# Three queues for the transfers of the last convolution: stores on SyncE and GpSimd, image loads on ScalarE

## The chip, the cores and the metric

The kernel runs on one core of one Trainium2 chip. The metric is the device time of one execution in microseconds (us), the median of several runs; smaller is better. A profiled execution gives the trace from which everything else is read.

## What is computed

The input x has 8 images of 16 channels of 256 x 256 float32. Four layers follow one another, each of the form x = x + f(gn(x)), where gn normalizes pairs of channels (8 groups of 2): a convolution with capsule routing, a convolution of splines, an attention over 16 x 16 patches, and last a 3 x 3 convolution with circular padding that the reference writes as a product of Fourier transforms. Only the last layer is touched here:

```
# --- layer 3 (conv_preact) ---
x = x + _L3_conv_ref(_gn(x), L3_conv_weight)
```

Because the padding is circular and the normalization is one factor and one offset for each image and channel, the layer is one convolution for each image: the factor goes into the weights, with 1 added at the centre for the residual, and the offset goes into a bias.

## The kernel before

The program is written instruction by instruction for each engine: TensorE (PE), VectorE (DVE), ScalarE (ACT), GpSimd (POOL) and SyncE (SP). A scheduler adds semaphores where one instruction needs another's result. In the last layer the order on each engine is the order of the program text (a manual schedule).

**Data.** The layer before writes its result to a scratch tensor in DRAM, `self.x3[b]`, one for each image `b`. `fetch3` (L1466) loads one image into an SBUF tile `xs` of 128 partitions x 33 x 258 floats with three DMAs: two of 2064 KB (L1471) and one of 32 KB (L1472). Three tiles take turns: `x30` (the profile calls it `pt`, since it is shared with the layer before) and two tiles `x3s`. Image 0 is loaded by SyncE during the layer before. Images 1 and 2 are loaded when the last layer begins, and image n + 2 into the tile of image n - 1, by an instruction that stands between the two halves of image n.

**Work.** For each image `n` there are two steps, s = 0 and s = 2; each step makes half of the image's rows and fills one tile `y` (`y3`, four buffers). In a step `products` (L1512) runs four times: q = 0 for k = 0 and 1, then q = 1 for k = 0 and 1. One such call is 48 products of 32 x 32 weights with 512 columns in float32, which the trace shows as 96 instructions MATMUL and 96 weight loads; a step is 384 of each. Two copies `seen` (L1583), one by ScalarE and one by VectorE, read the result of q = 0. `evict` (L1528) adds the bias and moves the result from PSUM to `y`: ScalarE takes k = 0 (L1537), VectorE takes k = 1 (L1535). The eight banks of PSUM are all in use in a step, so the products of the next step for k = 0 need ScalarE's eviction of this one.

**Stores.** `store` (L1539) writes the tile to the output. Partition 32c + 2o + r of `y` holds channel o of strip c (four strips of 64 rows), row parity r. For each c there are a DMA of 16 channels x 8 pieces of 2 KB (256 KB), one of 16 x 7 pieces of 2 KB (224 KB), and one of 16 x 2 rows of 1 KB (32 KB); in the step s = 2 the last of these for c = 3 is split in two of 16 KB because the image wraps around. So a step has 12 stores (s = 0) or 13 (s = 2), all issued by SyncE at one line, L1545.

**Waits.** A DMA signals its end on a semaphore. The DMAs of SyncE and ScalarE together use eight semaphores in rotation, those of GpSimd eight others; a DMA waits until the earlier one with its semaphore has landed.

The main loop, which sets the order:

```
for n, b in enumerate(images):
    for s in (0, 2):
        y = io.tile([P, 2, 2, 4, W], F32, name="y3", bufs=4)
        if s and n and n + 2 < len(images):
            xs.append(fetch(images[n + 2], xs[n - 1]))
...
        store(b, s, y)
```

Of the kernel before, what the change touches and what calls it, by code (L numbers as in the profile page):

```python
# [17 lines left out]
B, C, H, W = 8, 16, 256, 256  # L18
# [265 lines left out]
class _Net:  # L284
# [1189 lines left out]
    def layer3(self, images=range(B)):  # L1474
# [5 lines left out]
        nc, tc = self.nc, self.tc  # L1480
        with ExitStack() as st:
# [12 lines left out]
                return get  # L1494

            def fetch(b, xs):
                self.fetch3(nc.gpsimd, b, xs)
                return xs

            def weights(b):  # L1500
# [38 lines left out]
            def store(b, s, y):  # L1539

                y = y.rearrange("(c o r) s g j w -> r o c (s g j) w", c=4, r=2)

                def put(row, ap, src):
                    to = self.out[b, 0, row]
                    nc.sync.dma_start(out=bass.AP(tensor=to.tensor, offset=to.offset, ap=[[H * W, C], *ap]), in_=src)  # L1545

                row = 16 * s + 1
                for c in range(4):
                    for r, n in ((1, 8), (0, 7)):
                        put(  # L1550
                            row + 64 * c + 3 - 2 * r,
                            [[4 * W, n], [1, 2 * W]],
                            y[r, :, c, 1 - r : 1 - r + 2 * n].rearrange("o (m t) w -> o m (t w)", t=2),
                        )
                    if row + 64 * c + 31 < H:
                        put(row + 64 * c, [[31 * W, 2], [1, W]], y[0, :, c, 0:16:15])
                    else:
                        put(row + 64 * c, [[W, 1], [1, W]], y[0, :, c, 0:1])
                        put(0, [[W, 1], [1, W]], y[0, :, c, 15:16])
# [3 lines left out]
            xs = [self.x30.rearrange("p (g w) -> p g w", w=WP)]  # L1563
# [3 lines left out]
            with tc.manual_schedule():  # L1567
                for b in images[1:3]:
                    xs.append(fetch(b, io.tile([P, 33, WP], F32, name="x3s")))
# [5 lines that stand above are left out]
                        ps = [[psum.tile([P, 2, 512], F32, name="p3") for _ in range(2)] for _ in range(2)]  # L1575
                        for q in range(2):
                            for k in range(2):
                                products(s + k, q, ws, xs[n], ps[k])
                                if q:
                                    evict(b, s + k, ps[k], y)  # L1580
                                else:
                                    for h in range(2):
                                        (nc.vector.tensor_copy if k else nc.scalar.copy)(  # L1583
                                            seen[k][:, h], ps[k][h][:, :, 0]
                                        )
                        store(b, s, y)
                        if todo:
                            todo.pop(0)[2]()
                        while todo and todo[0][0] != "PE":
                            todo.pop(0)[2]()  # L1590
                        if s == 0 and n + 1 < len(images):
                            ws_after = weights(images[n + 1])
                    if n + 1 < len(images):
                        ws = ws_after
# [69 lines left out]
```

## Time and profile before

| what | value |
|---|---|
| median of 3 runs | 6713.02 us (6710.88 to 6718.76) |
| the profiled execution's own time | 6716.81 us |
| its span, first to last instruction | 6714.9 us |
| the last convolution in it, from the first product to the end | 6450.6 to 6714.9 us |
| TensorE busy over the span | 91% |
| mean granted TensorE clock | 0.985 |
| moved by DMA over the span | 800.86 MB |

The profiled execution lies 3.8 us over the median. Times inside it are counted from the start of the span. "PE" is TensorE's products, "PEld" its weight loads. "SPq" is the queue of SyncE's DMA instructions. The trace names DMA queues by number: q1 is SyncE's, q10 ScalarE's, q0 GpSimd's, and q8 brings the instructions of TensorE from DRAM. A row of the table by stretch of time has, in this order, the stretch and its length, the busy time and number of instructions of PE, PEld, DVE, ACT and POOL, the granted clock, the busy share of the 16 DMA engines and the GB/s moved.

### The profile page before, as it was taken

The page shows a single profiled execution, that of the slowest core. Times are in us where ns is not written, and L with a number is a line of the kernel's source. Part 1 is how long each engine was busy: PE and PEld are TensorE (multiplying, and loading weights), DVE is VectorE, ACT ScalarE, POOL GpSimd, SP SyncE. Part 2 cuts the span into 40 slices and gives each one's busy share as a digit, 9 for nine tenths or more (in the row PEclk, how much of TensorE's full clock was granted, in tenths as well). Part 3 has the DMA queues.
Part 4 walks back from the last instruction along what each step waited for, and adds up shares of the span by engine and source line. Part 5 has one row for each costly group of instructions (what it writes and reads, how often), then busy time and mean ns, then how long its engine had stood idle before and what let it go on. Part 6 is the DMA issues. An engine that isn't in the chain of part 4 may idle for free. (4 is left out here: it accounts for less than half of the span.)

```text
span 6714.9 us, 111421 instructions
## 1 busy us (share of the span) xinstructions
PE 6114.2 (91%) x46024; PEld 2770.4 (41%) x46024; DVE 5401.2 (80%) x6374; ACT 2737.7 (41%) x3898; POOL 3231.7 (48%) x2098
## 2 busy tenths in 40 slices
PE   3899899899988999899887799999999999999988
PEld 1333333333333333333333344444444466666655
DVE  5799999999999999999998899999999633333321
ACT  1333333333333333333332688888888421221211
POOL 0566666666666666666666444334344211111100
PEclk9999999999999999999998899999999999999999
DMA  6233333333333333333332555555556634344358
GB/s 260 61 87 90 92 90 93 90 88 91 91 90 91 89 88 88 88 88 88 88 88 61 171 177 176 175 176 178 175 174 175 177 87 94 81 93 95 91 173 222
DMA packets 375967, 800.86 MB, mean 119 GB/s; under 512 B 56210, under 2 KB 190386, under 8 KB 338210
## 3 DMA queue, kind: packets, MB, share of 16 engines
q1 hardware_dynamic: 339426, 730.09, 38.3%
q10 hardware_dynamic: 33792, 33.82, 1.5%
q0 software_dynamic: 2240, 29.82, 1.2%
q8 instruction: 361, 5.91, 0.4%
q14 instruction: 148, 1.21, 0.1%
HBM read 582.87 MB, written 210.77 MB: 118 GB/s over the span
## 5 line engine op out<-in xcount | busy, mean ns | idle before, releaser
L750 POOL TENSOR_TENSOR dd<-dd 128x1024 f32<-128x1024 f32 x512 | 1214.5, 2372 | 615.9 <-DVE dd L741 595.8
L1006 PE MATMUL ps<-bases,tw 128*32 128x512 f32 (+1 forms) x13824 | 1361.5, 545 | 18.2 <-POOL bases L975 7.9
L741 DVE SCALAR_TENSOR_TENSOR dd<-rb,v 128x1024 f32<-128x1024 f32 (+1 forms) x1024 | 1066.5, 1082 | 97.5 <-PE rb L730 91.0
L975 POOL TENSOR_TENSOR bases<-e,a 128x1024 f32<-128x1024 f32 (+1 forms) x264 | 621.8, 2378 | 930.9 <-DVE e L973 930.6
L629 DVE TENSOR_TENSOR pr<-v,fb 128x2048 f32<-128x2048 f32 (+1 forms) x512 | 1011.5, 2016 | 24.1 <-PE pl L639 12.8
L523 PE MATMUL cv<-kt,w 128*128 128x512 f32 x2048 | 1000.1, 610 | 28.2 <-DVE dd L741 21.4
L532 ACT COPY v<-cv 128x1024 f32<-128x1024 f32 x512 | 517.3, 1010 | 1151.7 <-PE cv L527 1151.7
L1006 PEld LDWEIGHTS ps<-bases,tw 128*32 128x32 f32 x13824 | 596.2, 109 | 804.9 <-issue 484.7
L750 POOL TENSOR_TENSOR s<-s,dd 128x512 f32<-128x512 f32 x512 | 671.4, 1311 | 35.0
L730 PE MATMUL rb<-rs,ct_fold 32*128 32x512 f32 x3584 | 608.9, 649 | 71.4 <-ACT rs L712 68.0
L750 POOL TENSOR_TENSOR s<-v,dd 128x512 f32<-128x512 f32 x256 | 330.3, 1290 | 659.8 <-DVE dd L741 659.8
L639 PE MATMUL pl<-pr,ct_fold 128*32 128x512 f32 x3584 | 534.2, 608 | 120.6 <-DVE pr L629 120.6
L527 PE MATMUL cv<-kt,w 64*128 64x512 f32 x2048 | 578.7, 641 | 0.0
L523 PEld LDWEIGHTS cv<-kt,w 128*128 128x128 f32 x2048 | 354.2, 190 | 524.9 <-issue 300.0
L1430 ACT ACTIVATE vt<-pv,w_b2v 128x128 f32<-128x128 f32 x512 | 146.5, 368 | 842.6 <-PE pv L1426 842.6
L1419 PE MATMUL pqk<-w_qk,t 128*128 128x512 f32 x1024 | 483.0, 594 | 4.6 <-POOL t L1413 4.6
L1451 DVE TENSOR_TENSOR y<-po,res 128x512 f32<-128x512 f32 x128 | 88.5, 692 | 490.8 <-PE po L1446 472.0
L983 DVE SCALAR_TENSOR_TENSOR bases<-xr,xm,bases 128x1024 f32<-128x1024 f32 (+1 forms) x264 | 447.8, 1734 | 0.3 <-POOL bases L975 0.3
L1413 POOL TENSOR_TENSOR t<-t,emb 128x512 f32<-128x512 f32 x128 | 162.3, 1268 | 507.2 <-DVE t L1409 496.5
L960 ACT ACTIVATE sq<-a 128x1024 f32<-128x1024 f32 (+1 forms) x264 | 263.7, 999 | 228.1 <-DVE a L952 227.3
L730 PEld LDWEIGHTS rb<-rs,ct_fold 32*128 32x128 f32 x3584 | 172.9, 185 | 415.6 <-issue 219.9
L942 ACT ACTIVATE d<-xr,bd,sd 128x1024 f32<-128x1024 f32 (+1 forms) x264 | 319.0, 1208 | 20.0 <-DMA xr<-x1p 20.0
(261 smaller groups left out, 8377.6 us busy)
## 6 DMA issues: line engine op xcount, KB each, us to landing
kt<-d SPq DMA_DIRECT2D x256, 516.0 KB
xr<-x1p SPq DMA_DIRECT2D x120, 1024.0 KB
d<-dn ACTq DMA_DIRECT2D x64, 516.0 KB
x<-y SPq DMA_DIRECT2D x128, 258.0 KB
xs<-in_x_dram SPq DMA_DIRECT2D x16, 2048.0 KB
xs<-in_x_dram SPq DMA_DIRECT2D x64, 512.0 KB
res<-in_x_dram SPq DMA_DIRECT2D x64, 512.0 KB
x<-s SPq DMA_DIRECT2D x128, 256.0 KB
```

The costliest lines, as they stand in the source:

```text
L523: nc.tensor.matmul(ps()[:, n], w[:, 0, j, :], t[:, a : a + 2, 0:W], start=True, stop=False)
L527: nc.tensor.matmul(ps()[:, n], w[at, 1, j, :], t[at, a : a + 2, 2 - n : 2 - n + W], start=False, stop=True)
L532: nc.scalar.copy(v[h]()[:, 4 * g : 4 * g + 4, j * W : j * W + W], ps().rearrange("p n (a w) -> p (n a) w", w=W),)
L629: nc.vector.tensor_tensor(pr()[:, :n].rearrange("p n (r w) -> p n r w", w=W), v[h]()[:, 4 * g : 4 * g + n].rearrange("p n (r w) -> p n r w ...
L639: nc.tensor.matmul(pl()[at : at + 32], sel[:, g, h, :], pr()[:, t, :], start=h == 0 and g == 0, stop=h == 1 and (g == 1 or t == 3),)
L730: nc.tensor.matmul(r()[:, n], spread[at, g, h, :], rs()[at], start=True, stop=True)
L741: nc.vector.scalar_tensor_tensor(dd()[:, :n], r()[:, :n], 1.0 / B, v[h]()[:, a : a + n], ALU.subtract, ALU.mult)
L750: op("POOL", us, lambda: nc.gpsimd.tensor_tensor(out[0](), a[0](), b[0](), ALU.add), a[1] + b[1], out[1])
L975: nc.gpsimd.tensor_tensor(ring[n % 3][:, 0, p : p + m, 1 : 1 + W], rows(e), rows(a), ALU.subtract)
L983: nc.vector.scalar_tensor_tensor(r, rows(part[1]), xm[:, b : b + 1], v, ALU.is_gt, ALU.mult)
L1006: nc.tensor.matmul(out if k is None else out[:, k], lhs, rhs, start=start, stop=stop, skip_group_check=True)
L1419: nc.tensor.matmul(ps, t[:, n, k * P : (k + 1) * P], wqk[:, n, :], start=n == 0, stop=n == 1)
```

## The change

SyncE keeps the stores of strips c = 0 and 1 (partitions 0 to 63 of `y`), GpSimd issues those of c = 2 and 3 (partitions 64 to 127). In the text they alternate (0, 2, 1, 3), so the two engines can issue at the same time. The loads of images 1 to 7, which GpSimd issued, are issued by ScalarE. SyncE has 6 stores in each step then, GpSimd 6 or 7: of 200 stores, 96 and 104. No compute instruction is added or removed.

```
             def fetch(b, xs):
-                self.fetch3(nc.gpsimd, b, xs)
+                self.fetch3(nc.scalar, b, xs)
                 return xs
...
                 def put(row, ap, src):
                     to = self.out[b, 0, row]
-                    nc.sync.dma_start(out=bass.AP(tensor=to.tensor, offset=to.offset, ap=[[H * W, C], *ap]), in_=src)
+                    (nc.sync if c < 2 else nc.gpsimd).dma_start(
+                        out=bass.AP(tensor=to.tensor, offset=to.offset, ap=[[H * W, C], *ap]), in_=src
+                    )
 
                 row = 16 * s + 1
-                for c in range(4):
+                for c in (0, 2, 1, 3):
                     for r, n in ((1, 8), (0, 7)):
```

## The prediction

> **What bounds the kernel now.** I read the table by stretch of time first, cut where an image load is issued (6450.3, 6483.9, 6519.75, 6554.4, 6585.0, 6617.0 us in the rows of L1471), then the chain of waits in one stretch, then the DMA queues in short windows. Three rows of the table: an image with a load beside it, one without, and the tail.
>
> ```profile
> 6484.00:6519.00 35.00, 31.44 (x776) 18.83 (x774) 7.18 (x15) 6.16 (x9) 1.48 (x3) 0.90 0.80 245
> 6647.00:6673.00 26.00, 25.84 (x780) 16.65 (x767) 6.11 (x9) 4.88 (x8) 0.00 (x0) 1.00 0.75 166
> 6702.00:6715.00 13.00, 0.00 (x0) 0.00 (x0) 0.00 (x0) 0.00 (x0) 0.00 (x0) 0.54 0.74 161
> ```
>
> PE sets the pace, and all other engines have room: 26 us an image without a load. The six images with a load take 34, 35, 35, 31, 32 and 30 us: 197 - 6 x 26 = 41 us lost. The granted clock falls there too (0.90). What stops PE is in the chain of waits from 6484 to 6519:
>
> ```profile
> 6493.74 4.47 PE p L1519 x122
> 6498.21 2.83 issue
> 6501.05 1.42 PE p L1519 x9
> ```
>
> "Issue" is a stop without a releaser, so neither an eviction nor a store holds PE. The packets of queue q8 (PE's instructions) explain it: one comes for every 128 products and 128 weight loads, some 3.9 us of work at full clock. From the crossing into a new block to the start of the next fetch I read 0.84 to 1.1 us with DMA idle, 2.0 to 2.8 under stores alone, 3.4 to 3.9 under a load alone, and 4.6 to 5.2 under both. PE goes on some 2.35 us after a fetch starts, so a delay over 3.9 - 2.35 = 1.6 us stops it.
>
> The DMA windows show what the transfers do. First, stores alone (6504 to 6514); second, stores just after a load (6497.5 to 6500.5):
>
> ```profile
> DMA packets 1149, 1.84 MB, mean 184 GB/s; under 512 B 193, under 2 KB 321, under 8 KB 1148
> q1 hardware_dynamic: 1148, 1.83, 81.6%
> ```
>
> ```profile
> DMA packets 691, 1.13 MB, mean 377 GB/s; under 512 B 123, under 2 KB 196, under 8 KB 688
> q1 hardware_dynamic: 658, 1.07, 94.4%
> ```
>
> The same queue, with like packets, moves 184 GB/s in one and 377 in the other. A 2-KB packet takes 152 ns where all 16 engines work on the same strip, and 84 ns where the load has left them out of step, on different strips. So issue is not the limit of the stores; what the engines read at one moment is. While a load runs, its 16-KB packets leave the stores a small share (6486 to 6497):
>
> ```profile
> q0 software_dynamic: 254, 3.93, 91.0%
> q1 hardware_dynamic: 159, 0.29, 6.9%
> ```
>
> Last, the tail: the last eviction by VectorE ends at 6698.98 + 2.48 = 6701.46, and the span at 6714.9. In between only 13 stores run: 2.10 MB from 6702.7 to 6713.3, 10.6 us at 198 GB/s.
>
> ```profile
> L1545 SPq DMA_DIRECT2D out_dram<-y x200: 577/613/2103, 6470.7 to 6711.3; - x100
> L1471 POOL DMA_DIRECT2D x3s<-x x10: 527/545/724, 6450.3 to 6617.5; - x10
> L1471 SPq DMA_DIRECT2D pt<-x x2: 452/502/552, 6358.5 to 6359.0; - x2
> ```
>
> Durations are ns, minimum/median/maximum. They are the prices of an issue on SP and POOL.
>
> **What the Trainium skill says.** "SBUF — State Buffer", "Door 1: The DMA port swizzle": 32 neighbouring partitions reach 8 of the 16 ports, the other half of the partitions uses the other 8, and 8 ports give some 218 GB/s. The 184 to 198 GB/s of stores alone agree. Its section "Can I just issue two DMAs to hit both halves?" found 6% only for two transfers from partitions 0 and 64. No window of before has that pair; the 377 GB/s shows that a mix of strips can go much faster than 218. "Runtime: NRT & Kernel Launch", "Instruction fetch mechanics": blocks of 16 KiB, 256 instructions, mostly hidden. The trace agrees on the size, not on the hiding (2.83 us above). "DMA: Bandwidth & Descriptors", "Issuing engines are not separate DMA queues": all share the same 16 engines, and more issuers save issue time only. The shares in 6486 to 6497 fit that.
>
> **The change part by part**, against the profiled execution's 6716.81 us (span 6714.9), which is 3.8 above the median.
>
> 1. *Tail.* SP issues 6 stores, 6 x 0.613 = 3.7 us; POOL 7 x 0.545 = 3.8 us (its price for DMAs of the same 128 descriptors; no trace shows POOL issuing stores). Both together are done before the data is. If the two queues make the engines read both halves, 2.10 MB take 5.6 us at 377 GB/s: 10.6 - 5.6 = 5.0 saved. If every engine alternates in step with the others, 6% is left: 0.6 saved. POOL at 1.5 us an issue would take 7 x 1.5 = 10.5 us and leave nothing. I take -5, bounds -5.2 and 0.
>
> 2. *Stores of the other 15 steps.* 90 issues leave SP and 97 come to POOL: 97 x 0.545 = 53 us of POOL, which in this layer works 1.5 us an image. Covered by that idleness; uncovered it is case R3. The cost is in PE's fetches. Now they pass one queue of stores and wait 2.0 to 2.8 us, which costs (26 - 6 x 3.9)/2 = 1.3 us a step. With two queues ahead, I estimate one more store's share, 1 to 1.5 us a fetch; if the burst is shorter (5.6 instead of 10.6 us), 1.5 instead of 2.7 fetches fall in it. So 1.5 x (1.8 + 0.5) = 3.5 at worst against 1.3 to 2.1 now. I take +0.4 a step, 15 x 0.4 = +6. Bounds: all of the present loss goes, -14 (short of 20, as a first fetch remains in every burst), or each of 2.7 fetches loses 0.9 more, 2.4 a step: +35.
>
> 3. *Loads, moved from POOL to ACT.* The 21 DMAs move past ACT's eviction of (n, 0): images 3 to 7 are requested at about 6497 instead of 6483.9, 11 to 13 us later. ACT issues three, 3 x 0.53 = 1.6 us by the nearest rows. Behind them on ACT stands `seen` of (n, 2), for which PE's products of the next step wait; between the two ACT idles 4.4 to 6 us, so 1.6 is hidden; without that cover 5 x 1.6 = 8. The first six loads precede the first `seen`, before which ACT idles 13 us. An image comes 8 to 22 us after issue and is needed some 40 us after: covered. On the 16 engines the load meets the stores of (n, 0) after 4 to 5 us, where now it meets those of (n-1, 2); the bytes are the same. I take +0.5 for each of six, +3, for the second store queue beside it. Bounds: loads on a queue of ACT's kind stop delaying fetches, -35 (most of the 41), or 2 us more for each, +13.
>
> 4. *Semaphores.* SP and ACT share eight, so a half load waits for a store and a later store waits for a half load. The stores in question are 13 us older; the store behind a load waits at most its 8 to 22 us, and `y` has four buffers, 52 us. The evictions wait for more semaphores, while PE has not finished anyway. I take 0, with +5 as the upper bound and no gain.
>
> Sum: -5 + 6 + 3 + 0 = +4: 6720.8 for a profiled execution, 6717 for the median of the runs shown.
>
> **Rivals.**
>
> *R1, slower: two store queues delay the fetch.* Place: PE's "issue" in all steps. For: the delay grew with each kind of traffic (1, 2.4, 3.6, 4.9 us). Against: a faster burst meets fewer fetches. Price: 15 steps x 2 us = +30, tail unchanged: 6743. It decides from a fetch delay of about 3.2 us under stores alone.
>
> *R2, faster: the engines see both halves everywhere.* A loaded image now needs 11 us for the load and 2 x 11 for stores, 33 us of DMA in 26 of PE, so nearly every fetch is delayed. At 377 GB/s it needs 11 + 2 x 5.6 = 22, a third less. A third of 41 is 14, half of the stores' 1.3 a step on 16 steps is 10, the tail 5: -29, 6684. For: the 377 window. Against: the 6% of the skill, and that fetches are worse in a denser burst.
>
> *R3: POOL's stores are slow to issue*, over 1.5 us each. Then the tail is 0 to 8 us longer and the bursts drag: 6713 to 6728.
>
> *R4: the change does not do what it says.* Issue was not the limit (377 GB/s came from SP alone), and engines in lockstep leave everything as it is: 6713.
>
> **How the numbers follow.** A measurement of this kernel can tell some 0.2%, 13 us, from no change. The near wash above has .40 and its own range 6703 to 6727 (same .33, slower .05, faster .02). R1 .31 (slower .29, same .02), R2 .22 (faster .21, same .01), R3 .04 (slower .03, same .01), R4 .03 (same). Sums: faster .23, same .40, slower .37. The range 6688 to 6748 takes in the wash, most of R1 and the near half of R2; about 2 in 10 lie beyond. The bounds added up (-54 to +53) lie further out and are not likely together.
>
> **What would show it right or wrong.** Tail: stores from about 6702.7 in two queues, together over 350 GB/s, or under 210 (then step 1 is wrong). Steps: the image without a load at 26 to 27 us; 28 or more is R1, under 25.5 R2. Loads: first packet 11 to 13 us later in an image, loaded images at 30 to 36 us; near 27 they no longer delay fetches. ACT: no wait of PE for `seen`; if there is one, issue on ACT was not hidden. POOL: issues at 0.55 us; over 1.5 is R3. The whole prediction fails if PE's stops no longer end with q8's packets.

## Result, and the profile after

The changed kernel takes 6727.86 us (median of 20 runs, 6720.73 to 6738.11), the kernel before 6714.91 us in the 20 runs beside them. The ratio is 1.0023, 95% interval 1.0016 to 1.003: slower by 0.23%, some 13 us. The forecast was 6717.0 with a range of 6688 to 6748, and "within 0.2%" as the likeliest case; the time lies in the range, just across the 0.2% line on the slow side.

The profiled execution took 6725.06 us, its span 6723.2. The last convolution runs there from 6444.65 us to the end, 278.6 us; before it was 264.4. (It begins 5.9 us earlier than in the trace of before. That is scatter of the three layers ahead, which the change does not touch; so all that follows counts from the first product of the layer.) I cut the layer at the end of VectorE's last eviction of each image:

| stretch | before, us | after, us | difference |
|---|---|---|---|
| image 0 | 35.4 | 41.0 | +5.6 |
| images 1 to 5 (five loaded images) | 164.0 | 167.9 | +3.9 |
| images 6 and 7 (no load) | 51.5 | 55.3 | +3.8 |
| tail, from the last eviction to the end | 13.5 | 14.3 | +0.8 |

Three rows of the table by stretch of time after the change: a loaded image, image 6, and the tail (the columns as in the table of before).

```profile
6588.00:6621.00 33.00, 27.89 (x749) 15.84 (x732) 5.85 (x9) 4.56 (x6) 6.33 (x12) 0.90 0.75 259
6653.60:6680.30 26.70, 25.93 (x791) 15.73 (x769) 6.12 (x9) 4.88 (x8) 6.94 (x13) 1.00 0.59 161
6709.00:6723.00 14.00, 0.00 (x0) 0.00 (x0) 0.00 (x0) 0.00 (x0) 3.71 (x7) 0.54 0.52 150
```

In image 6 the DMA engines are busy 0.59 of the time where they were 0.75 for the same bytes: the stores did become more efficient. The image is slower all the same. The chain of waits, in the stretch of images 6 and 7, shows where (start, length, what):

```profile
6648.79 12.93 PE p L1519 x352
6661.72 0.07 issue
6661.78 13.00 PE p L1519 x365
6674.78 0.71 issue
6675.49 12.93 PE p L1519 x353
6688.42 0.89 issue
6689.31 2.23 PE p L1519 x55
```

Before, PE ran 36.15 us on end in the same place (6662.74 to 6698.90). Now it stops about once a step. Each stop ends some 2.35 us after an instruction block of q8 begins to arrive, as before.

The tail. Most of the stores of the last step (1.73 of 2.10 MB) are in these 6 us, from the DMA queues in 6712 to 6718:

```profile
DMA packets 874, 1.73 MB, mean 289 GB/s; under 512 B 188, under 2 KB 280, under 8 KB 874
q0 software_dynamic: 397, 0.97, 61.0%
q1 hardware_dynamic: 477, 0.76, 33.5%
```

The two queues together move 289 GB/s, against 184 to 198 for SyncE's alone. The data takes from 6710.2 to 6718.2 us, 8.0 instead of 10.6. Yet the tail is no shorter. The rows of GpSimd's closing instructions and of SyncE's waits at the end (us in total, times, longest) say why:

```profile
L1662 POOLq DRAIN  x3: 40/98/10227, 6712.2 to 6723.0; - x3
SPq L1662 <- PEq L1662: 4.0, 2, 3.6
```

GpSimd's DRAIN at the end of the program starts at 6712.22, beside its last store, and lasts 10,227 ns, to 6722.44. Its last packet is at 6717.53; SyncE has seen every store land by 6719.1 and then waits 3.6 us for the common end. (The row names PE's queue, but the only instruction still under way is that DRAIN.) Before, GpSimd's DRAIN began at 6617.9, after the last load, and was long over.

The prices of issue came out as used:

```profile
L1545 POOL DMA_DIRECT2D out_dram<-y x104: 509/548/711, 6467.2 to 6712.7; - x104
L1471 ACTq DMA_DIRECT2D x3s<-x x10: 326/492/1288, 6444.1 to 6628.8; - x10
```

### The profile page after: what moved, and what is told of

It reads as the page before. It is cut to its first block, busy times and chain, and to the rows that moved or that the text cites. A ratio compares the mean times of both kernels' runs of the same rounds, so it can differ in the third digit from the quotient of the medians.

```text
span 6723.2 us, 111466 instructions
## 1 busy us (share of the span) xinstructions
PE 6116.5 (91%) x46024; PEld 2770.6 (41%) x46024; DVE 5401.4 (80%) x6374; ACT 2738.3 (41%) x3898; POOL 3275.4 (49%) x2181
## 5 line engine op out<-in xcount | busy, mean ns | idle before, releaser
L1006 PE MATMUL ps<-bases,tw 128*32 128x512 f32 (+1 forms) x13824 | 1361.5, 545 | 16.9 <-POOL bases L975 6.5
```

The lines of the kernel that those rows point to most:

```text
L1006: nc.tensor.matmul(out if k is None else out[:, k], lhs, rhs, start=start, stop=stop, skip_group_check=True)
```

## The delay of the instruction fetch, read over all runs

The prediction and its rivals turn on one quantity: the time from PE's crossing into a new block of 256 instructions to the start of the next q8 packet. I took it at 537 crossings of the layer in the 12 profiles with whole loads (before, after, and the ten experiments below that leave the loads in one piece), sorted by what else moved on the engines in that time:

| beside the fetch | fetches | mean delay, us | standard error |
|---|---|---|---|
| nothing | 85 | 1.01 | 0.03 |
| stores of SyncE | 233 | 1.83 | 0.04 |
| stores of GpSimd | 39 | 2.27 | 0.14 |
| stores of both at once | 56 | 2.85 | 0.14 |
| an image load | 41 | 3.95 | 0.06 |
| a load and stores of SyncE | 55 | 4.01 | 0.08 |
| a load and stores of SyncE and GpSimd | 28 | 4.44 | 0.10 |

The sorting is by what moved until the fetch came, so a long delay has more chance to meet a second kind of traffic. Sorted by the traffic of the first 0.8 us after the crossing alone, the three kinds of stores give 1.90, 2.65 and 2.91 us (standard errors 0.04, 0.19 and 0.16): the order stays, but GpSimd's stores alone are then close to both at once.

PE stops from about 1.6 us on. In images 6 and 7 the delays above 1.6 are 2.80, 2.19, 2.05 and 2.30 us before (excess 2.9 in sum) and 2.55, 1.86, 3.31, 3.55 and 4.27 after (excess 7.5). The difference, 4.6, is the size of the 3.8 us that these images lost. (The chain of waits shows less of it, because the ends of products are modelled in the trace: before, the block from 6666.76 us on took 4.57 us behind a delay of 2.2, others 3.9, and the chain has no stop there.) Over the whole layer the stops that the trace does show, in total, times and longest, are these, before and after:

```profile
PE p L1519 <- issue: 21.4, 16, 2.8
PE p L1519 <- issue: 30.7, 21, 2.8
```

Three of the experiments below leave the loads and all stores but those of the last step on their engines (the two under "The tail alone", and the one that changes only the order of the strips). There the stops are 18.0, 20.3 and 22.6 us, so the 9 us more are not scatter.

Image 0 has another cause. Its rows, before and after:

```profile
6450.57:6486.00 35.43, 32.02 (x821) 16.84 (x832) 7.00 (x13) 4.79 (x8) 4.70 (x9) 0.95 0.89 311
6444.60:6485.70 41.10, 36.00 (x828) 18.87 (x834) 7.01 (x13) 4.88 (x8) 3.39 (x6) 0.84 0.69 261
```

The same products keep PE busy for 36.0 instead of 32.0 us, at a granted clock of 0.84 instead of 0.95. As an estimate, the lower clock costs at most (1 - clock) x length: 1.8 us before and 6.6 after, so up to 4.8 of the 5.6 us. In images 1 to 5 it is the other way round, 0.94 before and 0.96 after (9.8 and 6.7 us), so the 3.9 us of the table can hide some 7. Where the clock falls differs from profile to profile. Its mean over the runs does not: 0.9845 in the 20 runs after, 0.9847 in 27 runs of the kernel before. So the clock explains most of image 0 in this one profile, and not the 13 us.

## Experiments

Theory A: the loss is the instruction fetch behind a second store queue, plus GpSimd's DRAIN. Theory B: it is the move of the loads. Ratios are to the kernel before, with 95% intervals.

**Each half of the change alone.** Loads only:

```
-                self.fetch3(nc.gpsimd, b, xs)
+                self.fetch3(nc.scalar, b, xs)
```

> Only the loads are moved to ScalarE; all stores stay on SyncE in their old order. Theory A (the loss comes from the second store queue: later instruction fetches in every step, and GpSimd's closing DRAIN): within 3 us of before, the slow steps move from s = 0 to s = 2 but are as long, the tail stays at 13.4 us. Theory B (the loss comes from the loads, which start half an image later and on another queue): +8 to +13 us, loaded images 33 us and more, images 6 and 7 unchanged at 25.5 us.

Measured: 6716.05, ratio 1.0003 (0.9994 to 1.0011). So B falls: the loads are not where the 13 us are. But the zero hides two changes. Images 1 to 5 took 157.3 us, 6.7 less than before, and the tail 20.1, 6.6 more. The waits of SyncE's queue explain the tail (us in total, times, longest); the shorter images are taken up at the end of this section.

```profile
SPq L1545 <- DMA x3s<-x: 31.3, 5, 9.3
SPq L1545 <- DMA pt<-x: 24.6, 4, 8.7
```

ScalarE's loads share the rotating semaphores with SyncE's stores, so nine times a store waited for a load to land, 55.9 us in all. SyncE's stores ended up behind: at the last eviction it was still issuing those of the step before. In the changed kernel SyncE has no such wait, with 6 stores a step.

Stores only (the store half of the diff; loads left on GpSimd):

> Only the stores are split; the loads stay on GpSimd, where they now stand behind GpSimd's stores of (n, 0). Theory A: +10 to +13 us, images 6 and 7 some 4 us longer together, tail 14.3 us with a closing DRAIN of 10 us on GpSimd. Theory B: not simply told apart, since the loads are late here too; but if it is ScalarE's queue that costs, +0 to +5 us.

Measured: 6734.69, ratio 1.0033 (1.002 to 1.0045). Image 0 took 40.9 us, images 6 and 7 57.8, the tail 15.3: all the loss, and more, comes with the split. (A part of the "more" can be the clock: its mean was 0.9838 in these six runs, 0.9847 in the runs beside them, some 6 us by the estimate above.) PE's stops in the layer are 31.5 us, as after the change. Theory A stands so far.

**The tail alone.** In both, only the last step's strips 2 and 3 leave SyncE, and that step's strips go in the order 0, 2, 1, 3:

```
-                    nc.sync.dma_start(...)
+                    (nc.gpsimd if c >= 2 and b == images[-1] and s else nc.sync).dma_start(...)
```

> Only the last step's stores are split over SyncE and GpSimd; all else as before. If GpSimd's closing DRAIN sets the end (after: last packet 6718.1, DRAIN to 6722.4): the stores take 8 instead of 10.6 us, the end comes 4 us after them, so 0 to +2 us. If the DRAIN is hidden: -3 us, tail 10.6 us.

Measured: 6712.26, ratio 0.9996 (0.9988 to 1.0004), tail 11.3 us, 2.2 shorter; in the whole time it can't be told from no change. The split does help the tail. Here the DRAIN ends 1.9 us after GpSimd's last packet, not 4.9, and SyncE's waits end only 0.6 us sooner than it.

> Only the last step's stores are split over SyncE and ScalarE; all else as before. If the second queue is what makes the stores faster and the DRAIN is GpSimd's alone: tail 10 to 11 us, -2.5 to -3.5 us. If two queues of the same kind stay in lockstep: no change, tail 13.4 us, 195 GB/s.

Measured, with ScalarE in GpSimd's place: 6733.11, ratio 1.003 (1.0018 to 1.0041), tail 29.9 us. Neither expectation held. SyncE's queue and the DMA queues in 6704 to 6708:

```profile
SPq L1545 <- DMA out_dram<-y: 24.3, 2, 23.8
```

```profile
DMA packets 435, 0.78 MB, mean 196 GB/s; under 512 B 51, under 2 KB 54, under 8 KB 435
q1 hardware_dynamic: 233, 0.44, 52.1%
q10 hardware_dynamic: 202, 0.34, 40.2%
```

SyncE stood 23.8 us, from 6678.6 to 6702.5, in the middle of an earlier step's stores. It went on when ScalarE's first store of the last step, issued at 6699.2, had had time to land. Both use semaphore 101, so I read it as the shared rotation making an early store of SyncE wait for a late one of ScalarE. While both queues did run, they moved 196 GB/s together. That does not answer the question that the run was made for: SyncE had stopped after six of the 13 stores of image 6's second half, so it was now sending that step's strips 2 and 3, while ScalarE sent strips 2 and 3 of the last step. Both read partitions 64 to 127. What SyncE and ScalarE would move from different halves is not shown by any run here, and neither is what SyncE and GpSimd would move from the same half; that the two halves make the 289 GB/s stays an argument.

**Two queues at once, or GpSimd's queue?** All stores on GpSimd, loads on SyncE:

> All stores are issued by GpSimd, one queue, which writes in 4-KB packets; the loads by SyncE. Theory A1 (the loss comes from two store queues ahead of the instruction fetch): images 6 and 7 back to 51 to 52 us together (before 51.5, after 55.3), fetch delays under stores at most 2.8 us. Theory A2 (it is GpSimd's queue or its 4-KB packets that delay the fetch): 55 us or more, delays over 3.2 us. Tail: the DRAIN on top of one queue's rate, 15 us or more if that queue stays near 200 GB/s.

Measured: 6729.37, ratio 1.0019 (1.0013 to 1.0026). Images 6 and 7 took 56.5 us with delays up to 3.61, with one store queue only, as A2 has it; PE's stops in the layer are 25.4 us, and the tail 16.9. A step's stores on one engine, SyncE and GpSimd in turn, loads on ScalarE:

> Loads on ScalarE; a step's stores are all on one engine, SyncE for s = 0 and GpSimd for s = 2, so both queues are used but not at the same time. A1 (two at once): images 6 and 7 at 51 to 52.5 us, total some 8 us below the changed kernel but for a longer tail. A2 (GpSimd's queue): the fetch is late in the steps after s = 2 alone, some 53.5 us.

Measured: 6731.6, ratio 1.0022 (1.0015 to 1.0028), images 6 and 7 57.6 us, tail 17.8. PE's stops in the layer are 31.1 us. A1 in its plain form falls: with the two queues in turn it is no better. GpSimd's burst alone (6662 to 6671, first) and SyncE's alone (6674 to 6684, second) in this kernel:

```profile
DMA packets 706, 1.89 MB, mean 210 GB/s; under 512 B 183, under 2 KB 199, under 8 KB 705
q0 software_dynamic: 705, 1.87, 88.3%
```

```profile
DMA packets 1130, 1.92 MB, mean 192 GB/s; under 512 B 160, under 2 KB 256, under 8 KB 1127
q1 hardware_dynamic: 1127, 1.88, 85.7%
```

Alone, GpSimd's queue is as slow as SyncE's, but carries the bytes in 705 packets instead of 1127: it joins two 2-KB pieces of a channel into one packet of 4 KB (median 299 ns, SyncE's 152). Of the delays in images 6 and 7, those during GpSimd's bursts were 2.58, 3.89, 2.86 and 3.66, those during SyncE's 2.44, 1.98, 2.62 and 2.41. In the table above GpSimd's queue in place of SyncE's adds 0.44 us to a fetch, and both at once 1.02; how much of the latter needs two queues is not settled, since these two kernels, which do not run both at once, lost as much in images 6 and 7 as the changed one.

**Is it the packet's length?** The changed kernel, with each piece of two rows stored as two rows by GpSimd:

```
+                    if c >= 2 and ap[-1][1] == 2 * W:
+                        for t in range(2):
+                            put(row + t, [ap[0], [1, W]], src[:, :, t * W : t * W + W])
+                        return
```

> The changed kernel, but GpSimd stores each piece of two rows as two rows in separate DMAs, so that its queue should write 2-KB packets (two rows of 1 KB of one channel) instead of 4-KB ones. Theory A2a (the length of its packets delays the fetch): fetch delays in images 6 and 7 fall from 3.3 to 4.3 us to 2.8 at most, the two images take 51.5 to 53 us (after 55.3), total 3 to 8 us below the changed kernel. Theory A2b (the queue as such, or the two together, whatever the packets): 55 us or more, delays over 3.2 us; no better than the changed kernel.

Measured: 6719.31, ratio 1.0006 (0.9998 to 1.0015), images 6 and 7 53.1 us. The time is near what A2a asks, but the premise failed: the queue now joined up to four 1-KB rows, and most of its packets were again 3 or 4 KB. The mean delay under both queues was 2.24 (20 fetches) in place of 2.82 (19) in the changed kernel, so something helped, and it was not a 2-KB packet. The length was tried properly on the loads, with the stores as before:

```
-                self.fetch3(nc.gpsimd, b, xs)
+                for k in range(0, 32 * WP, 4 * WP):
+                    nc.gpsimd.dma_start(out=at[:, k : k + 4 * WP], in_=rows[:, k : k + 4 * WP])
...
```

> The kernel before, stores untouched on SyncE; each image load is cut into pieces of 4 rows (8 DMAs of 516 KB and the one of 32 KB, all on GpSimd), so that its packets are 4,128 bytes instead of 16,512. If the length of the packets in front of the instruction fetch sets its delay: under a load alone 2.0 to 2.8 us instead of 3.95 (mean of 41 fetches in the profiles so far), loaded images at 29 to 31 us, total -8 to -20 us. If the delay comes from the traffic as such: 3.5 us and more, total -3 to +3 us.

Measured: 6709.41, ratio 0.9991 (0.9984 to 0.9997). This is faster than both kernels, by 5.5 us against before. Delays: 3.41 under a load (5 fetches) and 3.61 under a load and stores (11), so shorter, but not the 2.0 to 2.8 of the theory. Images 1 to 5 took 156.8 us (before 164.0). But by the estimate above up to 6.7 of these 7.2 us are the granted clock, 0.98 in these images and 0.94 before. PE's stops in the layer are 20.3 us, within the 18.0 to 22.6 of the kernels with whole loads. Over all runs, too, the mean clock was higher, 0.98538 in 21 runs against 0.98464 in the 33 of before beside them, which is worth some 5 us: nearly the whole gain. So it is not shown that the kernel is faster because of the shorter delays; why its clock was higher stays open. The load beside nothing, 6490 to 6494, keeps most of its rate (386 to 410 GB/s before):

```profile
DMA packets 389, 1.46 MB, mean 365 GB/s; under 512 B 35, under 2 KB 35, under 8 KB 389
q0 software_dynamic: 389, 1.46, 98.5%
```

> As e16_load_4rows with pieces of 2 rows: 16 DMAs of 258 KB, packets of 2,064 bytes, as long as SyncE's store packets. If length sets the delay: 1.8 to 2.2 us under a load, loaded images at 27 to 30 us, total -10 to -25 us, less whatever the smaller packets cost the load's rate; GpSimd issues 17 x 0.54 = 9 us a load and is idle. If it does not: -3 to +5 us.

Measured: 6711.37, ratio 0.9995 (0.9987 to 1.0003). The packets were not 2 KB but again 4,128 bytes: GpSimd's queue joined pairs. The delays were 2.65 (3 fetches) and 3.09 (20), but the load fell to 305 GB/s (6484.5 to 6488.5) and lay beside the stores longer. Both runs together: 3.27 us (31 fetches) under a load and stores, against 4.01 with whole loads. So a shorter packet in front shortens the delay; packets of a quarter of the length took away 0.7 us, and the rest stays. What that is worth in the kernel's time can't be told apart from the clock, whose mean was 0.98538 here too.

**The other tries.** Only the order of the strips on SyncE:

> Only the order of the strips is changed to 0, 2, 1, 3, all stores on SyncE, loads on GpSimd. All theories: no change beyond 0.1%, 195 GB/s in the tail, because one queue's engines go through one strip after the other in step. If neighbouring DMAs overlap enough to use both halves: tail 3 to 5 us shorter.

Measured: 6717.27, ratio 0.9999 (0.9991 to 1.0008), tail 13.3: as expected, neighbours do not overlap enough to shorten it. Two attempts to keep the shorter images of e1_loads_act without its backlog, by giving strips 2 and 3 of the last image, or of the last step alone, to GpSimd:

> Loads on ScalarE as in e1_loads_act, all stores on SyncE, except those of strips 2 and 3 of the last image, which GpSimd issues. In e1 the steps of images 1 to 5 took 157.3 us (before 164.0), and the tail 20.2 us (before 13.4), since SyncE had fallen behind with its stores. If that backlog is all that hid the gain: tail 11 to 13 us, total -5 to -8 us against before. If the shorter steps were chance: no better than before.

Measured: 6713.16, ratio 0.9994 (0.9986 to 1.0003); images 1 to 5 took 153.5 us, the tail 12.1, but images 6 and 7 60.0, with one delay of 5.51 us where the backlog of SyncE met GpSimd's stores.

> Loads on ScalarE and stores on SyncE as in e1_loads_act; of the last step alone strips 2 and 3 go to GpSimd, the only DMAs it has in this layer. Images 1 to 5 at 153 to 158 us, images 6 and 7 at 52 us as in e1 (GpSimd's stores come after PE's last product), tail about 16 us instead of e1's 20.1 since 1.05 MB of the backlog goes beside the rest; a short DRAIN after the last packet, 1 to 2 us. Total -2 to -5 us against before. If the tail stays at 20 us: 0 to +2.

Measured: 6714.42, ratio 0.9998 (0.999 to 1.0007); images 1 to 5 157.4 us, images 6 and 7 56.2 (not 52), tail 14.3. The backlog only moved. The shorter loaded images are in all three kernels with ScalarE's loads and SyncE's stores (157.3, 153.5, 157.4; 161.1 to 164.0 in the four with GpSimd's whole loads and SyncE's stores). That the held-up stores no longer run beside the load can be a reason, but it is not shown: PE's stops in these images are 14.1, 13.9 and 17.1 us there and 14.7 to 20.3 in the four, less than 3 us apart on average, and the clock was 0.96, 0.99 and 0.98 against 0.93 to 0.97.

## Why the prediction was right, and where its sum was off

- **The range**, 6688 to 6748, is wide: R1 at its full price (6743) lies in it too. That the time fell inside says little of the sum, which was 9 us too low, most of it in step 1.
- **The bound** was right: PE paced by its instruction fetch, stopped by what is on the DMA engines. Nothing else became the bound.
- **Step 1, tail: -5 taken, bounds -5.2 and 0; measured +0.8.** The first half was half right: 2.6 us saved on the data, since the pair reached 289 GB/s and not 377, and SyncE ran alone for the first 1.3 us. (That the 377 came from engines on different strips was a reading; no view tells which engine reads which strip.) The second half was missing: GpSimd's DRAIN, 3.6 us after all stores had landed. The bounds looked at issue and at data, not at how the program ends. This term alone is 5.8 of the 9 us between the predicted +4 and the measured +13.
- **Step 2, store bursts: +6 taken (+0.4 a step); measured +3.8 in the four steps of images 6 and 7, about +1 a step**, and some 7 in the ten steps of images 1 to 5 with the clock taken out as estimated (the loads had moved there too). The added delay was right: 1 to 1.5 us estimated, 1.02 measured. The saving was overrated: the burst is shorter, but still about one fetch of every step falls into it, and that one costs on average 1.5 us beyond the limit in images 6 and 7. The cause was also half missed: a part of the delay, 0.44 us or more, comes with GpSimd's queue even alone.
- **Step 3, loads: +3 taken; the move alone changed the total by 0.0003 of 6715, +2 us (interval -4 to +7)**, well inside. Issue on ScalarE was hidden, as costed: it stood in the idle time ahead of `seen`. The 41 us that the prediction put down to the fetches beside loads hold a part that is the lower clock, some 10 us in images 1 to 5.
- **Step 4, semaphores: 0 taken, right for this kernel.** In the kernels that split the work otherwise, the same sharing cost 6.6 us in the tail and 16 us (tail 29.9 instead of 13.5); the bound of +5 was too low for those.
- **The rivals.** R1 had the right place and the right side, at half its price: mean delay 2.85, not the 3.2 from which it was to decide, 1 us a step, not 2. Its cause, two queues, is only in part the right one: GpSimd's queue without SyncE's delays the fetch as well. R2 did not come: one queue stays near 200 GB/s, and a denser burst cost more than it freed. R3 fell: 0.548 us an issue. R4 fell: the two queues moved 289 GB/s, and the time changed.

The Trainium skill, "DMA: Bandwidth & Descriptors", section "Queues, rings and completion order", says that an engine takes the queues that have work in turn and finishes a packet of one before it goes to the next. A packet is there some 9 to 17 descriptors; whether the trace's packets are the same is not shown here. The delays agree in direction: 1.01, 1.83 and 2.85 us with no, one and two store queues, and shorter with shorter load packets. They do not agree with length alone, for 4-KB load packets still cost more than 3 us and 4-KB store packets of GpSimd 2.27. "SBUF — State Buffer", "Can I just issue two DMAs to hit both halves?", gives 6% for two transfers from partitions 0 and 64. Here SyncE and GpSimd gained half as much again (289 GB/s against 184 to 198): for this pair the measurement decides.

What stays open: why GpSimd's queue delays a fetch more; why the by-row stores helped though their packets stayed long; why the clock was higher with loads in pieces; and what sets how long GpSimd's DRAIN outlasts its last packet. It was 4.9, 5.0 and 6.0 us with 104, 104 and 125 DMAs on GpSimd in the program, 1.1 to 1.9 with 7 to 28, but 3.1 with 63, 1.0 with 119, 2.8 with 168 and 3.9 with 200, so the number of DMAs is not it.

## What to carry to other kernels

Where TensorE is bound and its instructions come from DRAM, look at what lies on the DMA engines when it crosses into a new block: faster transfers in more queues can cost more there than they save. Before DMAs go to GpSimd at the end of a program, count its closing DRAIN; before they are spread over SyncE and ScalarE, look at the semaphores that the two share. The one kernel here that was clearly faster than the one before, by 5.5 us, cut the largest transfers into pieces of a quarter. The fetch delay fell by 0.7 us, but the gain came with a higher granted clock: before a stretch of one profile is explained, compare the clock of that stretch, and its mean over all runs.

## What the hardware showed that was not expected

- GpSimd's queue joins neighbouring pieces of a partition into packets of about 4 KB (two of 2,048, four of 1,024, two of 2,064 bytes); SyncE's and ScalarE's do not.
- Stores: 289 GB/s for SyncE and GpSimd together from the two halves of the partitions, 184 to 210 for either alone, 196 for SyncE and ScalarE together from one half. The 377 GB/s of one queue just after a load stand in the prediction.
- GpSimd's DRAIN ends 1.0 to 6.0 us after its last packet, and the program's end waits for it where that packet comes late.
- In one kernel, image 0 of the last layer had a granted clock of 0.84 where another had 0.95 for the same products, worth up to 4.8 us, while the means over their runs were 0.9845 and 0.9847.
